# A four-layer convolution kernel: routing of the first seven images issued inside the last image's layer 2

## The chip, the core and the metric

The kernel runs on one core of one Trainium2 chip. A core has TensorE (PE in the profile, with its weight loads shown apart as PEld), VectorE (DVE), ScalarE (ACT), GpSimd (POOL) and SyncE (SP, which here only issues DMAs). Each engine takes its instructions in the order of its own queue and waits on semaphores for the others. The metric is the device time of one execution in microseconds (us); lower is better.

## What is computed

Eight images of 512 channels and 32 x 32 pixels, all in float32, go through four layers:

```
x = L0(x)   # group norm, 8-head attention, 3 steps h += 0.1*tanh(h W), projection, residual
x = L1(x)   # attention over all 1024 pixels, 64-wide q and k, residual
x = L2(x)   # upsample by 2 (12-tap FIR), leaky ReLU, downsample by 2 (12-tap FIR)
pooled = x.mean(axis=(2, 3))
rw = sigmoid(pooled @ router_w.T + router_b)            # 8 experts per image
W  = einsum('be,eoihw->boihw', rw, experts)             # each image has its own weights
x = relu(bn3(conv3(relu(bn2(conv2(relu(bn1(conv1(x, W1))), W2))), W3)) + x)
```

conv1 is 1x1 (512 to 128 channels), conv2 3x3 (128 to 128), conv3 1x1 (128 to 512). The change concerns the line with `rw`, the routing: from an image's pooled means to eight numbers that weigh the experts.

## The kernel before

Layers 0, 1 and 2 run image by image, for b = 0 to 7. Layer 3 then runs image by image over the results. Those of images 0 to 6 were spilled to DRAM at the end of their layer 2 and are loaded back by `load_z`; that of image 7 stays in SBUF.

The source gives the order in which work is issued; a scheduler then places every instruction in its engine's queue by its priority (earlier in the source is higher) and by the time at which it believes that its operands are there. So an instruction may stand in its queue well ahead of older work that is still waiting for something. Once placed, the order is fixed, and an instruction that waits holds up all that stand behind it on the same engine. Semaphores are put in automatically.

Layer 2 of an image works in eight strips t = 0 to 7 of up to nine input rows. Layer 1 writes its result `y` to a padded DRAM buffer (`ypad`, line 764: most of these DMAs are issued by ACT, the others by SP), and `halo` (line 880, SP) reads overlapping patches back. `upsample(t)` (line 920) makes four matmuls with 512 columns; each is two passes on PE in float32. `leak` follows each of them: an ACT multiplication into a small buffer (line 903), then a DVE maximum into `up` (line 904). There are two such buffers. `downsample` (line 941) makes many small matmuls on `up`. It is called three times: after strips 0 to 2, after 3 and 4, and after 5 to 7. The first call's result is copied to `z` by ACT (line 955), the second's by DVE (lines 957 and 958), the last one's by both (lines 960 and 961), and DVE then sums `z` into `pooled` (line 962).

For image 7 alone, layer 2 gets a callback, `freed(t)`, called at the end of each `downsample` with its last strip (2, 4 and 7) and with 6 ahead of the last one. Before, it does nothing for t = 2. At 4 it issues the load of the experts `w2_0` and of image 0's `z`, at 6 those of `w2_1` and `w2_2` (called w_0e, w_1e and w_2e in the profile, and w_0, w_1, w_2 here), at 7 that of `w3`. Each of these goes into a big buffer that the work just ended gives free. The experts `w1` have a buffer of their own and are loaded before.

`route(b0, b1)` (lines 1050 to 1076) computes `rw` for images b0 to b1 - 1: DVE scales `pooled` into `mean` (line 1054); PE makes four tiny matmuls `router` (line 1057, eight passes); DVE spreads the result into `apart` (line 1063); PE makes one matmul `routed` that brings it to all partitions (line 1068); DVE adds the bias (line 1072); ACT takes the sigmoid (line 1076), for which it first loads a function table. `route(0, B - 1)` is called right after its definition, ahead of image 7's layer 2 in the source. Image 7's own routing, `route(B - 1, B)`, comes behind that layer.

`mixed(b)` (lines 1087 to 1099) makes an image's weights in five parts (w1, w_0, w_1, w_2, w3): ACT multiplies the first expert (line 1094), and seven DVE steps of line 1096 add the others; a step of w1 or w3 has 512 elements per partition, one of w_0 to w_2 has 384. There are two buffers for these weights, so those of images 0 and 1 can be made as soon as their `rw` and the experts are there. The scheduler does that: `mixed(0)` and `mixed(1)` stand far behind in the source, but their w1 parts are placed as early as `rw` allows.

In layer 3 (lines 1128 to 1175) each image has matmuls c1 (line 317), c2 (line 1150) and c3 (line 1164); DVE's line 1171 takes each result of c3 out of PSUM into `z`. The pair of PSUM banks of one c3 chunk is free for the chunk after next once that has run.

Of the kernel before, what the change touches and what calls it, by code (L numbers as in the profile page):

```python
# [18 lines left out]
B, C, H, W = 8, 512, 32, 32  # L19
# [25 lines left out]
def tile_conv_sequence(tc: tile.TileContext, a: dict, out: bass.AP):  # L45


    redo = tile_sequence(tc, a, out, False)
    with tc.If(redo > 0):
        tile_sequence(tc, a, out, True)  # L50
# [3 lines left out]
def tile_sequence(ctx: ExitStack, tc: tile.TileContext, a: dict, out: bass.AP, shifted: bool):  # L54
# [15 lines left out]
    def bank(pool=None, name="mm"):  # L70
        pool = pool or ps_mm
        return pool.tile([P, HALF], F32, tag="bank", name=name)
# [823 lines left out]
    def layer2(b, halo, freed=lambda t: None):  # L896
# [32 lines left out]
        def downsample(first, last, ts_):  # L929
            for cc in range(CC):  # L930
# [28 lines left out]
                else:  # L959
# [3 lines left out]
                    if b + 1 < B:  # L963
                        nc.sync.dma_start(spilled[b][ts(cc, P), :], z[:, cc, :])
            freed(ts_[-1])

        for t in range(3):
# [10 lines left out]
        up63 = tmp(f"up63_{b}")[0 : 2 * W, :]  # L978
        leak(up63, ps, f"{b}_63")
        freed(6)  # L980
        downsample(17, 31, (5, 6, 7))
        return z
# [34 lines left out]
    def load_experts(key, n, pool=None):  # L1017
        if pool is None:
            t = big_tile(f"{key}e", [P, NE, n])
        else:  # L1020
            t = pool.tile([P, NE, n], F32, name=f"{key}e", bufs=1)
        nc.sync.dma_start(t, a[key])
        experts[key] = t

    def load_z(b):
        t = big_tile(f"z3_{b}", [P, CC, S])
        for cc in range(CC):
            nc.sync.dma_start(t[:, cc, :], spilled[b][ts(cc, P), :])
        return t
# [20 lines left out]
    def route(b0, b1):  # L1050

        n = b1 - b0
        mean = pool3.tile([P, CC, n], F32, name=f"mean_{b0}", bufs=1)
        nc.vector.tensor_scalar_mul(mean, pooled[:, :, b0:b1], 1.0 / S)
        ps = bank(ps_tp, f"router_{b0}")
        for cc in range(CC):
            nc.tensor.matmul(
                ps[0:n, 0:NE], mean[:, cc, :], router_w[:, cc, :],
                start=(cc == 0), stop=(cc == CC - 1),
            )  # L1060

        apart = pool3.tile([n, n, NE], F32, name=f"apart_{b0}", bufs=1)
        nc.vector.tensor_tensor(
            apart, ident[0:n, 0:n].unsqueeze(2).to_broadcast([n, n, NE]),
            ps[0:n, 0:NE].unsqueeze(1).to_broadcast([n, n, NE]), ALU.mult,
        )
        ps = bank(ps_tp, f"routed_{b0}")
        nc.tensor.matmul(
            ps[:, 0 : n * NE], ones[0:n, :], apart.rearrange("k b e -> k (b e)"),
            start=True, stop=True,  # L1070
        )
        nc.vector.tensor_tensor(
            rw[:, b0:b1, :], ps[:, 0 : n * NE].rearrange("p (b e) -> p b e", e=NE),
            router_b.unsqueeze(1).to_broadcast([P, n, NE]), ALU.add,
        )
        nc.scalar.activation(rw[:, b0:b1, :], rw[:, b0:b1, :], AF.Sigmoid)

    route(0, B - 1)


    rims = []
    for i in range(2):
        t = pool3.tile([P, H + 2, W + 2], F32, tag=f"rim_{i}", bufs=1, name=f"rim_{i}")
# [30 lines left out]
    z3 = {}  # L1114

    def freed(t):
        if t == 4:
            load_experts("w2_0", 3 * P)
            z3[0] = load_z(0)
        elif t == 6:  # L1120
            for ky in (1, 2):
                load_experts(f"w2_{ky}", 3 * P)
        elif t == 7:
            load_experts("w3", C)

    z_last = layer2(B - 1, halo, freed)
    z_next = z3[0]
    redo = None if shifted else out_of_bounds()
# [115 lines left out]
```

## Time and profile before

Four runs took 3938.16, 3941.11, 3941.77 and 3942.65 us; their median is 3941.44 us. The profiled execution took 3942.35 us, with a span of 3940.6 us from its first to its last instruction.

| | busy us | share of the span | instructions |
|---|---|---|---|
| PE | 3872.7 | 98% | 14630 |
| PEld | 2037.3 | 52% | 14630 |
| DVE | 2594.5 | 66% | 3690 |
| ACT | 1105.1 | 28% | 1507 |
| POOL | 435.5 | 11% | 310 |
| mean granted TensorE clock | 0.996 of full speed | | |

How to read it: PE is busy nearly all the time, so the span is PE's work plus its idle time, and an average says little about one stage. What matters here is the short stretch from about 3609 us, where image 7's layer 1 ends, to about 3750 us, in layer 3. In a row of the timeline, the first number is the start in us, the second the time to the end of the group, then engine, line, operation, tiles, shapes and count; in brackets stands how long the engine idled before it, and what ended that.

### The profile page before, as it was taken

Reading aid. Unit: us, or ns where it says so; the run is one execution under the profiler, and the core shown is the slowest. Engines: PE = TensorE matmul, PEld = TensorE weight load, DVE = VectorE, ACT = ScalarE, POOL = GpSimd, SP = SyncE. Lnnn points to the kernel's source line nnn. Section 1 sums busy time; section 2 is a strip of 40 time slices with the busy share of each in tenths; the row PEclk is TensorE's granted clock in tenths of the full one; section 3 lists DMA queues with packets and bytes.
Section 4 is the critical chain, followed back from the end, with each engine's and each line's share of the span. In section 5 each row is a group of like instructions: output and inputs, shape, how many; then the busy total and the mean of one; then the engine's idle time right before and its main releaser. Section 6 shows DMA issues by size and latency. Waiting matters only on the chain.

```text
span 3940.6 us, 37957 instructions
## 1 busy us (share of the span) xinstructions
PE 3872.7 (98%) x14630; PEld 2037.3 (52%) x14630; DVE 2594.5 (66%) x3690; ACT 1105.1 (28%) x1507; POOL 435.5 (11%) x310
## 2 busy tenths in 40 slices
PE   8999999999999999999999999999999999999998
PEld 4336653476435763366434764357534764346543
DVE  4777848764686647775586646765477655866785
ACT  1421224212332114212242123322142122421333
POOL 5310003000120003100030002200030001201000
PEclk9999999999999999999999999999999999999999
DMA  5002310122101310023101220013200131003432
GB/s 196 19 0 83 111 61 1 40 75 101 38 0 59 117 70 8 0 83 115 56 1 59 82 77 37 1 71 105 78 1 30 57 113 55 1 0 115 161 135 101
DMA packets 85792, 247.86 MB, mean 63 GB/s; under 512 B 10480, under 2 KB 33024, under 8 KB 78816
## 3 DMA queue, kind: packets, MB, share of 16 engines
q1 hardware_dynamic: 69712, 220.23, 15.7%
q10 hardware_dynamic: 13824, 12.59, 1.0%
q0 software_dynamic: 2064, 12.51, 0.8%
q8 instruction: 117, 1.92, 0.2%
q14 instruction: 75, 0.61, 0.0%
HBM read 185.40 MB, written 59.90 MB: 62 GB/s over the span
## 4 chain that ended last, share of the span: by engine, by line
PE 90%; DVE 7%; issue 1%; DMA 1%; ACT 1%; SPq 0%; POOL 0%; DVEq 0%; ACTq 0%; POOLq 0%
PE scores L266 13%; PE av L627 11%; PE inl_X L414 6%; PE dn L941 6%; PE up L920 5%; PE v_X L414 4%; PE inl_Y L414 4%; PE av_X L854 4%; PE c L1150 3%; PE v_A L414 3%; PE v_Y L414 3%; PE inl_A L414 3%; PE av_A L854 3%; PE av_Y L854 2%; PE proj_X L414 2%; PE q_X L414 2%
## 5 line engine op out<-in xcount | busy, mean ns | idle before, releaser
L612 ACT ACTIVATE e<-scores 128x1024 f32<-128x1024 f32 x512 | 497.0, 1021 | 632.7 <-PE scores L266 632.0
L618 DVE TENSOR_TENSOR acc<-acc,e 128x1024 f32<-128x1024 f32 x384 | 494.4, 1287 | 122.8 <-ACT e L612 101.7
L266 PE MATMUL scores<-q,k 64*128 64x512 f32 x2048 | 511.1, 616 | 6.9 <-ACT e L612 3.6
L627 PE MATMUL av<-e,v 128*64 128x512 f32 x2048 | 494.2, 605 | 0.0
L644 POOL TENSOR_TENSOR seen<-seen,acc 128x512 f32<-128x512 f32 x128 | 212.1, 1657 | 1578.8 <-DVE acc L618 1573.8
L266 PEld LDWEIGHTS scores<-q,k 64*128 64x128 f32 x2048 | 175.9, 186 | 334.2 <-ACT e L612 163.2
L627 PEld LDWEIGHTS av<-e,v 128*64 128x64 f32 x2048 | 124.8, 136 | 338.7 <-issue 335.7
L941 PEld LDWEIGHTS dn<-dn_op,up 128*128 128x128 f32 (+1 forms) x2048 | 241.7, 193 | 47.0 <-issue 24.3
L904 DVE SCALAR_TENSOR_TENSOR up<-up,leak 128x512 f32<-128x512 f32 (+1 forms) x264 | 175.1, 687 | 137.6 <-ACT leak L903 128.9
L941 PE MATMUL dn<-dn_op,up 128*128 128x126 f32 (+5 forms) x2048 | 246.7, 276 | 10.6 <-DVE up L904 9.9
L903 ACT ACTIVATE leak<-up 128x512 f32<-128x512 f32 (+1 forms) x264 | 150.0, 595 | 251.8 <-DVE up L904 127.2
L641 DVE RECIPROCAL inv<-total 128x512 f32<-128x512 f32 x64 | 214.7, 3355 | 0.0
L920 PE MATMUL up<-halo,up_op 126*128 126x512 f32 (+1 forms) x384 | 184.8, 611 | 0.4 <-DVE up L904 0.3
L414 PE MATMUL inl_X<-T_hf,w_inl 128*128 128x512 f32 x384 | 172.6, 592 | 0.0
L644 POOL TENSOR_TENSOR seen<-seen,inv 128x512 f32<-128x512 f32 x64 | 125.2, 1956 | 417.8 <-DVE inv L641 417.8
L414 PE MATMUL inl_A<-hf,w_inl 128*128 128x512 f32 x384 | 169.6, 595 | 0.0
L616 DVE TENSOR_TENSOR acc<-e,e 128x1024 f32<-128x1024 f32 x64 | 84.9, 1327 | 102.3 <-ACT e L612 100.6
L508 ACT ACTIVATE inl_U<-inl_U,inl_b 128x512 f32<-128x512 f32 x96 | 64.0, 714 | 304.7 <-DVE inl_U L523 304.7
L519 DVE TENSOR_TENSOR inl_U<-inl_X,inl_P 128x512 f32<-128x512 f32 x96 | 61.9, 686 | 115.9 <-PE inl_X L414 115.9
L736 POOL TENSOR_TENSOR seen<-seen,acc 128x512 f32<-128x512 f32 x16 | 22.6, 1411 | 1019.9 <-DVE acc L728 1019.9
L1150 PE MATMUL c<-rim,mixed 128*128 128x512 f32 x288 | 124.9, 592 | 0.0
L414 PEld LDWEIGHTS inl_A<-hf,w_inl 128*128 128x128 f32 x384 | 72.4, 190 | 94.4 <-issue 88.7
(302 smaller groups left out, 5764.7 us busy)
## 6 DMA issues: line engine op xcount, KB each, us to landing
halo<-ypad_u SPq DMA_DIRECT2D x128, 252.0 KB
halo<-ypad_u SPq DMA_DIRECT2D x128, 198.0 KB
w_v<-stored_u_v SPq DMA_DIRECT2D x14, 1792.0 KB
x<-in_x_dram SPq DMA_DIRECT2D x32, 512.0 KB
spill_u<-z SPq DMA_DIRECT2D x28, 512.0 KB
z<-spill_u SPq DMA_DIRECT2D x28, 512.0 KB
out_dram<-z SPq DMA_DIRECT2D x28, 512.0 KB
w_q<-stored_u_q SPq DMA_DIRECT2D x7, 1792.0 KB
```

The lines of the kernel that those rows point to most:

```text
L266: nc.tensor.matmul(ps[r], k[r], q[r], start=True, stop=(shift is None))
L414: nc.tensor.matmul(dst, lhs, rhs, start=(opens and s == 0 and cc == 0), stop=(cc == 1 and s == rows), skip_group_check=True,)
L612: nc.scalar.activation(e, ps, AF.Exp, scale=HD ** -0.5)
L618: nc.vector.tensor_add(accs[g], accs[g], e)
L627: nc.tensor.matmul(avs[g][rows[r]], v[:, jc, ts(2 * oc + r, HD)], e[:, ts(r, HALF)], start=(jc == 0), stop=(jc == SC - 1),)
L641: nc.vector.reciprocal(inv, ps)
L644: nc.gpsimd.tensor_add(seen, seen, part)
L854: nc.tensor.matmul(ps[:, ts(s, QR)], left[:, j, at : at + P], right[:, j, :], start=(what in ("P1", "U2", "W") and s == 0 and j == 0), sto ...
L904: nc.vector.scalar_tensor_tensor(dst, ps, SQRT2, t, ALU.mult, ALU.max)
L920: nc.tensor.matmul(ps[i], op[0 : IR * n, :], halo.tile(t)[0 : IR * n, c + i, :], start=True, stop=True,)
L941: nc.tensor.matmul(rows[:, r0 - first : r1 + 1 - first, c0 : c1 + 1], up[t][0:k, c, ts(cc, P)], op[:, r0 - 4 * t + 3 : r1 + 4 - 4 * t, c0 ...
L1150: nc.tensor.matmul(banks[g].rearrange("p (h w) -> p h w", w=W), wt[:, at : at + P], h1[:, ky + 16 * g : ky + 16 * g + 16, kx : kx + W], st ...
```

## The change

The call of `route` for images 0 to 6 is taken from its place behind the definition and put into the callback, under t = 2, that is behind the first `downsample` of image 7's layer 2.

```diff
         nc.scalar.activation(rw[:, b0:b1, :], rw[:, b0:b1, :], AF.Sigmoid)
 
-    route(0, B - 1)
-
 
     rims = []
@@
     def freed(t):
-        if t == 4:
+        if t == 2:
+
+            route(0, B - 1)
+        elif t == 4:
             load_experts("w2_0", 3 * P)
             z3[0] = load_z(0)
         elif t == 6:
```

`route` itself is unchanged. No operation is added or removed: the eight passes of `router`, the two of `routed`, three DVE instructions and the sigmoid with its table load are issued later. What depends on `rw`, the steps of `mixed(0)` and `mixed(1)`, is placed anew by the scheduler. In the queues that result:

- PE: `router` stood between the last matmuls of layer 1, right ahead of the first upsampling, and `routed` a few matmuls behind it. Now `router` stands between the first `downsample` and `upsample(3)`, and `routed` behind the first matmul of `upsample(3)`. The matmuls of the second `downsample` are interleaved otherwise with those of `upsample(4)` to `upsample(6)`. In layer 3, image 7's `router` stands behind all eight c1 matmuls of image 0, where it stood behind five; image 0's third and fourth c3 chunks stand behind seven of image 1's eight c1 matmuls.
- DVE: 14 steps of line 1096 for w1 (seven each of images 0 and 1) stood among the last instructions of layer 1, eight of them directly ahead of the first `leak` of layer 2. Now none stands ahead of that `leak`; between the first `leak` of strip 3 and the `mean` of image 7's routing stand ten of them, with all seven w_0 steps and all seven w_1 steps of image 0 and four of its w_2 steps. The other four w1 steps, and all of image 1's w_0 steps, stand behind that `mean`.
- ACT: the table load and the sigmoid stood ahead of two writes of `ypad`. Now they stand behind the four copies of line 955, ahead of the first `leak` of strip 3.
- SP: two writes of `ypad` stand one `halo` load earlier. POOL: the same order.

## The prediction

> **What bounds the kernel now.** I read the page first: the chain that ended last is 90% PE, so a change counts by what it does to PE's idle time or pace. Next the waits of PE:
>
> ```profile
> engine line waited for: us in total, times, longest us
> PE dn L941 <- DVE up L904: 9.9, 7, 5.6
> ...
> PE up L920 <- DMA halo<-ypad_u: 2.4, 2, 1.5
> ```
>
> Over half of the 9.9 us is one wait. The timelines of DVE and PE around it say where (two engines of one window):
>
> ```profile
> 3627.11 0.88 DVE L817 SCALAR_TENSOR_TENSOR y<-av_P,inv,y 128x256 f32<-128x256 f32 x2
> 3627.91 5.63 DVE L1096 SCALAR_TENSOR_TENSOR mixed<-w1e,rw,mixed 128x512 f32<-128x512 f32 x8
> 3633.46 0.68 DVE L904 SCALAR_TENSOR_TENSOR up<-up,leak 128x512 f32<-128x512 f32 x1
> ```
>
> ```profile
> 3625.45 3.13 PE L920 MATMUL up<-halo,up_op 126*128 126x512 f32 x6
> 3634.19 1.12 PE L941 MATMUL dn<-dn_op,up 112*128 112x66 f32 x4 [5.61 <-DVE up L904]
> 3635.61 3.78 PE L920 MATMUL up<-halo,up_op 126*128 126x512 f32 x4 [0.29 <-DVE up L904]
> 3639.18 1.92 PE L920 MATMUL up<-halo,up_left_op 99*128 99x512 f32 x2
> 3640.89 3.30 PE L920 MATMUL up<-halo,up_op 126*128 126x512 f32 x6
> ```
>
> Eight weight-mixing steps stand ahead of image 7's first leak on DVE. PE ends the upsampling that it can do and idles 5.61 us. Then it is slow: four passes with 512 columns take 3.78 us. The windows show why (length, then busy us and counts of PE, PEld, DVE, ACT, POOL; granted clock; DMA share and rate):
>
> ```profile
> 3625.00:3634.00 9.00, 3.46 (x9) 1.25 (x7) 8.93 (x15) 0.00 (x0) 0.00 (x0) 0.88 0.56 177
> 3634.00:3644.00 10.00, 9.51 (x16) 4.54 (x17) 5.49 (x9) 4.64 (x9) 0.00 (x0) 0.60 0.78 267
> 3644.00:3654.00 10.00, 10.00 (x91) 9.97 (x90) 1.98 (x3) 3.20 (x6) 0.00 (x0) 1.00 0.26 83
> ```
>
> After the idle, the granted clock is 0.60 over ten microseconds. If it is half or full, that is 8 us at half. The same stretch of image 6, which has no mixing steps:
>
> ```profile
> 3166.99 2.85 PE L920 MATMUL up<-halo,up_op 126*128 126x512 f32 x6
> 3169.67 0.56 PE L941 MATMUL dn<-dn_op,up 112*128 112x66 f32 x4
> 3170.07 1.93 PE L920 MATMUL up<-halo,up_op 126*128 126x512 f32 x4
> ...
> 3178.36 8.73 PE L941 MATMUL dn<-dn_op,up 128*128 128x126 f32 x76 [0.89 <-DVE up L904]
> 3186.92 1.05 PE L920 MATMUL up<-halo,up_left_op 99*128 99x512 f32 x2
> ```
>
> Here the downsampling follows the six passes at once, and four passes take 1.93 us.
>
> **The change, term by term.** U is the start of strip 3's upsampling on PE: 3654.28 in image 7, 3186.92 in image 6.
>
> *(a) Ahead of the stall.* `router` (0.35 us, PE at 3609.88) goes from a place where PE idles next for 1.46 us until a halo patch lands; the patch sets the start, 3611.69, so this gains nothing. `routed` (3616.18, next matmul 3616.53) stood between busy matmuls: -0.35 us. On ACT the two `ypad` writes no longer wait for the sigmoid (3617.13), but `y`, which they carry, is written at 3617.01 to 3617.89: nothing either. SP's shift by one load (0.85 us) concerns patches of strip 3, used 20 us later.
>
> *(b) The stall.* From the six passes to U: image 7 takes 3654.28 - 3625.45 = 28.83 us. The same instructions take 18.77, 19.33, 20.07, 19.24 and 19.93 us in images 1, 2, 3, 5 and 6 (U minus the start of the six passes), mean 19.47. Image 4 takes 22.59 (rivals). After the change image 7 has the same instructions there: -9.36 us, bounds -8.8 and -10.1. By parts: 5.61 idle; 3634.19 to 3635.61 against 3169.67 to 3170.07, 1.02 more; twelve passes in 3635.61 to 3644.03, 8.42 us against 5.34 in image 6, 3.08 more; together 9.7, less the short waits (0 to 0.9) that images 1 to 6 have later. Nearly 4 us of this is no wait but half rate.
>
> [...]
>
> *(c) Routing at its new place.* `router` and `routed` now stand between busy matmuls: 0.25 (eight passes about 0.03 apart) and 0.35 us, +0.6. PE's trip over DVE to `routed` is covered by the first upsampling matmul (0.86). ACT's table load (1.28) runs behind the last z copy, while PE waits on neither; the sigmoid waits for `routed` and DVE's addition, and strip 3's first leak stands behind it. Leak starts at U + 1.94 now (3656.22) and some 0.3 later then; PE has seven more passes to do: +0.05.
>
> *(d) Fourteen w1 steps elsewhere.* Interleaved they are 0.665 us apart (four in 2.73), in all 9.3 us on DVE. Their cover has to be DVE's idle time in layer 2:
>
> ```profile
> 3656.85:3696.26 39.41, 38.76 (x214) 27.36 (x213) 32.50 (x59) 16.01 (x30) 0.00 (x0) 1.00 0.54 194
> ...
> 3696.26:3720.72 24.46, 24.45 (x65) 10.50 (x64) 23.25 (x42) 5.20 (x8) 0.00 (x0) 1.00 0.27 110
> ```
>
> The first row runs from strip 3's first leak to image 7's `mean`; DVE is busy 32.50 of 39.41 us. Its list changes by +10 w1, +3 w_2 and -4 of image 1's w_0 (0.53 each): 6.65 + 1.6 - 2.1 = +6.1 us, against 6.9 us idle. Set one by one in the new order, the steps fill about 4 us of that idle (the 0.66 us waits of DVE on ACT above all) and push `mean` back about 2.1 us, to U + 44.5 with the 0.3 of (c). PE wanted it for `router` at U + 43.47 (3697.75); it now has three more c1 matmuls ahead (3 x 0.86) and the 0.6 of (c): U + 46.6. It waits for nothing, by about 2 us. Next, `routed` of image 7 comes five c2 matmuls (4.3 us) later; DVE then needs 4 x 0.665 + 3 x 0.53 = 4.25 us to reach `apart`: the same slack. The first w3 step moves from `mean` + 4.2 to `mean` + 1.2, while w3e lands at U + 44.8 (3699.10) and ACT's first step takes 0.7: ready at U + 45.5, wanted at U + 45.7, so DVE may idle a few tenths. Last, DVE's way from `mean` to c3's first result (3718.86, U + 64.6) grows by four w1 and four w_0 steps of image 1 less three w_2 of image 0, 3.2 us, less its 1.2 idle: with the 2.4 above, U + 69.0, and 1.28 for itself. PE wants the banks that it frees after four c3 and seven c1 matmuls, 11 x 0.86 behind U + 62.4 (3716.67) + 0.6: U + 72.5. From the third image DVE has 2 to 3 us idle in each 29.5 us and catches up. Bounds: 0 and 9.3 us. I take +0.4, near the lower end, since every place has slack by these rows.
>
> Sum: -0.35 - 9.36 + 0.65 + 0.4 = -8.66 us. Against the profiled execution's 3942.35 that is 3933.7; it lies 0.91 above the median of the runs, 3941.44, which gives **3932.8 us**.
>
> **Rivals.**
> 1. *Half the clock gain is missing.* Image 4 had waits of 0.92 and 0.89 us at U - 11.6 and - 10.2, and its 76 small matmuls took 10.36 instead of 8.73 us. If image 7 gets such a dip, (b) is 28.83 - 22.59 = 6.24, and the time 3932.8 + 3.1 = 3935.9. For it: image 7's strip patches land as late as image 4's. Against: one image of six. A run of before that escaped the half rate (3938.16 may be one) would show the same smaller gain, but three of four lie above 3941. [...]
> 2. *DVE becomes the late engine at one of the three places of (d)*, costing 3 to 5 us: about 3937. For: it is 95% busy in the second row above. Against: the slack worked out.
> 3. *Slower: DVE takes the stall over.* If the filled idle is not there, all 9.3 us meet PE at `router` or `routed` of image 7; a wait that long halves the clock again, +3.6: 3932.8 - 0.4 + 9.3 + 3.6 = 3945.3. It decides once `mean` is later than U + 46.6 by more than about 8 us. Against: it needs all the idle time to stay unused, though the steps stand between the leaks.
> 4. *The stall stays*, because the first leak waits for something else just behind the steps: 3941.4. Against: in images 1 to 6 the leak follows `y` on DVE at once (3166.97 + 0.80 = 3167.77).
>
> **Chances and range.** Forecast 0.67 (3930.5 to 3935), rival 1 0.12, rival 2 0.12, rival 3 0.06, rival 4 0.03. A difference of 0.2%, 7.9 us, is about what a measurement of this kernel can tell from no change; it lies 0.8 us inside the forecast, which I put beyond it four times in five: faster 0.54. Within: the rest of the forecast, rivals 1, 2 and 4 and a third of 3: 0.42. Slower by more: 0.04, if the delay of rival 3 also reaches image 1. The range reaches over rivals 1 and 2: 3929 to 3938.5.
>
> **What would show it.** In the profile after: no wait above 1 us of PE's L941 on DVE's L904 at image 7; granted clock 1.00 over the ten microseconds behind that place; about 19.5 us from the six passes to U; `router` between the 92 small matmuls and U; DVE above 95% busy from U to layer 3's second image; no PE wait above 1 us at image 7's `router` and `routed`, at L1150 or at the third c3 chunk of image 0. It is wrong if the clock dips there again, if L904 still comes late, or if a wait of several us appears at the start of layer 3.

## The result, and the profile after

The changed kernel takes 3932.05 us (median of 32 runs, 3927.23 to 3937.61). The kernel before, over all of its 52 runs, takes 3939.95 us (3932.88 to 3948.08). The ratio is 0.9981, with a 95% interval from 0.9976 to 0.9986: 5.5 to 9.5 us less (the medians differ by 7.90), where the prediction had 8.66. (It was made against the 3941.44 us of the four runs shown; against 3939.95 the same sum gives 3931.3.) The profiled execution took 3931.28 us, with a span of 3929.5.

PE's waits in the changed kernel, by the line that waited and what it waited for (the same view as before):

```profile
engine line waited for: us in total, times, longest us
...
PE dn L941 <- DVE up L904: 2.4, 4, 0.9
...
PE up L920 <- DMA halo<-ypad_u: 2.3, 2, 1.8
```

The 5.6 us wait of the first downsampling is gone; no wait of L941 on a leak is above 0.9 us. PE's timeline from image 7's first patch to strip 3:

```profile
3607.59 1.10 PE L920 MATMUL up<-halo,up_left_op 99*128 99x512 f32 x2 [1.80 <-DMA halo<-ypad_u]
...
3622.67 2.93 PE L920 MATMUL up<-halo,up_op 126*128 126x512 f32 x6
3625.44 0.56 PE L941 MATMUL dn<-dn_op,up 112*128 112x66 f32 x4
3626.55 1.99 PE L920 MATMUL up<-halo,up_op 126*128 126x512 f32 x4 [0.55 <-DVE up L904]
...
3632.05 10.51 PE L941 MATMUL dn<-dn_op,up 112*128 112x84 f32 x92
3642.48 0.35 PE L1057 MATMUL router<-router_w,mean 128*7 128x8 f32 x8
3642.76 1.12 PE L920 MATMUL up<-halo,up_left_op 99*128 99x512 f32 x2
3643.82 0.42 PE L1068 MATMUL routed<-apart,ones 7*128 7x56 f32 x2
3644.17 2.84 PE L920 MATMUL up<-halo,up_op 126*128 126x512 f32 x6
```

The downsampling follows the six passes at once, four passes take 1.99 us instead of 3.78, and `router` stands between the 92 small matmuls and U, the start of strip 3. From the six passes to U it is 3642.76 - 3622.67 = 20.09 us instead of 28.83. DVE around the same place shows why:

```profile
3623.60 0.88 DVE L817 SCALAR_TENSOR_TENSOR y<-av_P,inv,y 128x256 f32<-128x256 f32 x2
3624.40 0.68 DVE L904 SCALAR_TENSOR_TENSOR up<-up,leak 128x512 f32<-128x512 f32 x1
```

The leak follows the last `y` with no mixing step between. The windows behind (columns as before) have the clock at 1.00, where before had 0.60:

```profile
3625.00:3634.00 9.00, 8.45 (x35) 4.83 (x34) 6.22 (x11) 5.72 (x11) 0.00 (x0) 1.00 0.78 254
3634.00:3644.00 10.00, 10.00 (x88) 9.11 (x88) 1.26 (x3) 3.45 (x6) 0.00 (x0) 1.00 0.81 262
```

The two profiled spans differ by 11.07 us, more than the medians do. Three stretches add up to it. Up to image 7's first upsampling matmul (3611.69 before, 3607.59 after) nothing was changed but that `router` no longer stands just ahead of it, in a wait of PE, and the 4.10 us there are chance: in e1 to e6 of the experiments this point, with the same work ahead of it, lies anywhere from 3605.65 to 3615.40. From there to U, which I call the ruler below, before takes 42.59 us and after 35.18 (the last digit is rounded in the rows): 7.41 less. From U to the end it is 286.28 and 286.73: 0.45 more. So the change itself gave 6.96 us in this pair of profiles.

### The profile page after: what moved, and what is told of

Read it like the earlier page. It is cut to its first block, busy times and chain, and to the rows that moved or that the text cites. A ratio compares the mean times of both kernels' runs of the same rounds, so it can differ in the third digit from the quotient of the medians.

```text
span 3929.5 us, 37961 instructions
## 1 busy us (share of the span) xinstructions
PE 3870.4 (98%) x14630; PEld 2034.6 (52%) x14630; DVE 2593.1 (66%) x3690; ACT 1105.1 (28%) x1507; POOL 435.6 (11%) x310
## 4 chain that ended last, share of the span: by engine, by line
PE 91%; DVE 6%; issue 1%; DMA 1%; ACT 1%; SPq 0%; POOL 0%; ACTq 0%; DVEq 0%; POOLq 0%
PE scores L266 13%; PE av L627 11%; PE inl_X L414 6%; PE dn L941 6%; PE up L920 5%; PE v_X L414 4%; PE inl_Y L414 4%; PE av_X L854 4%; PE c L1151 3%; PE v_A L414 3%; PE v_Y L414 3%; PE inl_A L414 3%; PE av_A L854 3%; PE av_Y L854 2%; PE proj_X L414 2%; PE q_X L414 2%
## 5 line engine op out<-in xcount | busy, mean ns | idle before, releaser
L941 PEld LDWEIGHTS dn<-dn_op,up 128*128 128x128 f32 (+1 forms) x2048 | 241.8, 193 | 40.2 <-issue 25.2
L941 PE MATMUL dn<-dn_op,up 128*128 128x126 f32 (+5 forms) x2048 | 246.2, 276 | 3.1 <-DVE up L904 2.4
L854 PE MATMUL av_X<-v,eT 128*128 128x256 f32 x512 | 120.6, 384 | 1.8 <-DVE av_W L833 1.0
```

Source lines behind the costliest of these rows:

```text
L854: nc.tensor.matmul(ps[:, ts(s, QR)], left[:, j, at : at + P], right[:, j, :], start=(what in ("P1", "U2", "W") and s == 0 and j == 0), sto ...
L941: nc.tensor.matmul(rows[:, r0 - first : r1 + 1 - first, c0 : c1 + 1], up[t][0:k, c, ts(cc, P)], op[:, r0 - 4 * t + 3 : r1 + 4 - 4 * t, c0 ...
```

## The experiments

"Half-clock record" in the expectations means a stretch for which the trace records the granted clock at 0.5. Within one profile such records start on multiples of 3.413 us from each other (the last section has the places); the stretch of 3.41 us from one such multiple to the next is called a window here.

### What makes the stall: the mixing steps or the routing itself

e1 leaves the routing at its old place and holds only the mixing: the steps of `mixed` read `rw_held`, a copy of `rw` that waits for image 7's first downsampled rows (a column of them, times zero, is added). In the code shown here, `@@` stands for lines left out.

```diff
     route(0, B - 1)
@@ def mixed(b):
+        rwb = rw_held if b < B - 1 else rw
@@ layer2, behind each downsample
+            if b == B - 1 and first == 0:
+                n = (B - 1) * NE
+                nc.vector.scalar_tensor_tensor(
+                    rw_held[:, 0 : B - 1, :].rearrange("p b e -> p (b e)"),
+                    z[:, CC - 1, 0:n], 0.0,
+                    rw[:, 0 : B - 1, :].rearrange("p b e -> p (b e)"), ALU.mult, ALU.add,
+                )
             freed(ts_[-1])
```

> The routing of images 0 to 6 is called where it was before the change; only the weight mixing is held: it reads a copy of rw that DVE makes from image 7's first downsampled rows (times zero, added). Ruler: from image 7's first upsampling matmul to U, the start of strip 3's upsampling (before 42.59 us, after 35.17 us, of which about 1.3 us stand under one half-clock record of 3.41 us). Theory (the mixing steps on DVE alone make the stall): 33.2 us (13.76 of before up to the six passes, with routed inline, plus 19.47), up to 34.9 with one half-clock record; no PE wait above 1 us on a leak; time 3929 to 3935, as after. Rival A (the place of router, routed or the table load matters by itself): the 5.6 us wait is still there, ruler 42.6, time about 3940.

Measured: 3930.8 us against 3939.41 of the kernel before, ratio 0.998 (0.997 to 0.9989). PE's timeline of e1:

```profile
3607.14 0.35 PE L1065 MATMUL router<-router_w,mean 128*7 128x8 f32 x8
3608.93 1.10 PE L920 MATMUL up<-halo,up_left_op 99*128 99x512 f32 x2 [1.43 <-DMA halo<-ypad_u]
...
3622.68 2.93 PE L920 MATMUL up<-halo,up_op 126*128 126x512 f32 x6
3625.45 0.56 PE L941 MATMUL dn<-dn_op,up 112*128 112x66 f32 x4
...
3642.40 1.04 PE L920 MATMUL up<-halo,up_left_op 99*128 99x512 f32 x2
```

The ruler is 33.48 us (33.2 expected) with `router` at its old place. So the stall is the mixing steps' alone, and rival A falls. The row of `router` shows one thing more: there it fills part of the patch's wait, and PE idles 1.43 us instead of the 1.80 in the changed kernel.

### How much of it was the clock

e2 gives PE something to do in the old stall. DVE keeps its 14 steps; the extra results are overwritten.

```diff
+                if b == B - 1 and first == 0 and cc == 0:
+                    for _ in range(6):
+                        nc.tensor.matmul(ps, up_op[0 : IR * IC, :],
+                            halo.tile(1)[0 : IR * IC, 2, :], start=True, stop=True)
                 blocks = [(t, c) for t in ts_ for c in range(4)]
```

> The kernel before, with six more upsampling matmuls of 512 columns (each two passes, 6 x 0.86 = 5.2 us) that write the bank of image 7's first downsampling, whose own first matmul then starts it anew: PE has work in the 5.61 us, DVE is as before. Theory (nearly 4 of the 9.4 us are the clock at half, brought about by PE's idle time): no half-clock record near image 7's first downsampling, ruler 42.59 - 3.1 to 3.6 = 39.0 to 39.5 us, time 3936.5 of a median 3940. Rival B (the passes behind the stall are slow for another reason, such as the patches' transfers at a DMA share of 0.78): ruler 42.2 to 42.6 us, time as before.

PE's timeline of e2 (its L936 are the added passes, L947 is the downsampling):

```profile
3623.65 1.02 PE L920 MATMUL up<-halo,up_op 126*128 126x512 f32 x2
...
3627.09 4.45 PE L936 MATMUL dn<-halo,up_op 126*128 126x512 f32 x10
3632.40 0.66 PE L947 MATMUL dn<-dn_op,up 112*128 112x66 f32 x4 [0.85 <-DVE up L904]
3633.81 1.99 PE L920 MATMUL up<-halo,up_op 126*128 126x512 f32 x4 [0.76 <-DVE up L904]
```

From the first of the six passes to the first downsampling it is 3632.40 - 3623.65 = 8.75 us, in before 3634.19 - 3625.45 = 8.74: the stall on DVE is untouched, but PE is busy 7.90 us of these 8.75, at a granted clock of 1.00. Yet from that downsampling to the end e2 takes 302.14 us (3934.54 - 3632.40) and before 306.36 (3940.55 - 3634.19), and no half-clock record lies there. Transfers are no cause: in the ten us behind, their share is 0.80 in e2 and 0.78 in before. So 4.22 us of the price were the half rate (3.1 to 3.6 expected), brought about by PE's own idle time; PE's wait behind that downsampling is even 0.47 us longer in e2 (0.76 against 0.29). The ruler itself is no measure for e2, since the scheduler put U ahead of a part of the small matmuls; and the timed median, 3937.35 against 3939.41 (ratio 0.9993, 0.9983 to 1.0003), can't tell the 4 us from nothing. This reading rests on the two profiles.

### The price of a shorter stall

e3 and e4 lengthen the first leak of the changed kernel.

```diff
+            for _ in range(3 if name == f"{B - 1}_0_0" else 1):   # e4: 5
                 nc.vector.scalar_tensor_tensor(dst, ps, SQRT2, t, ALU.mult, ALU.max)
```

> The changed kernel; image 7's very first leak on DVE is issued three times instead of once (same operands, same result), 2 x 0.665 = 1.33 us more ahead of the first downsampling. Theory: some 0.3 us are covered, PE idles 0.9 to 1.1 us, the clock stays at full; ruler (35.17 - 1.3 for the half-clock record of after = 33.9) 34.9 us. Rival C (any wait near 1 us halves the clock, as the two of 0.9 us in image 4 did): 36.6 us with a record of 3.41 us.

> As the last, with four more leaks, 2.66 us. Theory (the clock halves where PE was idle over half of a free-running window of 3.41 us; the records of before and after start at multiples of 3.413 us from each other): PE idles 2.3 us, ruler 36.2 us at full clock, and in about two of three cases one record of 3.41 us more, 37.9 us. Rival D (a stall always brings three windows, 10.24 us, as before): 39.8 us. Rival E (the price is the idle time alone): 36.2 us and no record in any case.

| | DVE work added | from the six passes to U | PE idle in it | half-clock record behind |
|---|---|---|---|---|
| after | 0 | 20.09 | 0.55 | none |
| e3 | 1.33 us | 22.91 | 0.98 + 0.76 | 3.41 us |
| e4 | 2.66 us | 24.19 | 2.43 + 0.76 | 3.41 us |
| before (no `router` in it) | eight steps | 28.83 | 5.61 + 0.29 | 10.24 us |

e4 came out as the theory had it (ruler 37.59, 37.9 expected). e3 did not: 36.30, close to rival C's 36.6, where I expected 34.9. I had counted the first wait alone. The windows of e3 on both sides of the halving:

```profile
3629.27:3632.68 3.41, 1.71 (x7) 1.09 (x8) 2.15 (x4) 1.56 (x3) 0.00 (x0) 1.00 0.85 260
3632.68:3636.09 3.41, 3.41 (x6) 1.30 (x5) 2.67 (x4) 2.08 (x5) 0.00 (x0) 0.50 0.79 266
```

In the first of them PE is busy 1.71 us of 3.41, because the waits of 0.98 and 0.76 us both fall into it; the next runs at half throughout. So two more leaks, 1.33 us, cost 2.82. Rival D (always three windows) and E (idle time alone) fall with e4. Single runs, 3937.22 and 3941.11 us, say little here: both had 6.83 us at half clock in image 5 (from 2721.32 and 2723.91), in code that no edit touches.

### How much room DVE has for the steps

e5 and e6 issue the routing later still, behind the second and behind the last downsampling.

```diff
     def freed(t):
-        if t == 2:
-            route(0, B - 1)
-        elif t == 4:
+        if t == 4:              # e6: t == 7, behind load_experts("w3", C)
+            route(0, B - 1)
```

> The changed kernel, with the routing of images 0 to 6 issued behind image 7's second downsampling instead of the first, ahead of the loading of w2_0. Rulers: from image 7's first upsampling to U (after 35.18 us with a half-clock record, held mixing 33.48 without), and from U to the end (286.3 to 286.7 in before, after and the held mixing). Theory (DVE has some us of idle time left in layer 2 and at the start of layer 3, and they run out if the steps come later): first ruler 33.2 (34.6 with a record), the second 289, 2.3 us more, by setting the steps one by one in the new order; PE waits of 1 us and more where image 7's layer 2 ends. Rival F (there is room wherever the steps stand): second ruler 287.0 or less. Rival G (all 14 steps show, 9.3 us): 296.

> The same with the routing issued behind image 7's last downsampling, so that none of the mixing lies in layer 2. Theory: PE waits some 8 us for mixed_0 at the first c1 matmul of layer 3 and some 2 us at image 0's third c3 chunk, the clock halves behind the first, second ruler 286.5 + 12.3 + 3 to 4 = 302 us, time 3946 to 3949, slower than the kernel before. Rival F: second ruler 287, time 3931.

e5: ruler 33.12, from U to the end 289.34 (289 expected); 3930.14 us in one run. PE's timeline at the end of image 7's layer 2 in e5:

```profile
3671.75 0.68 PE L949 MATMUL dn<-dn_op,up 64*128 64x96 f32 x4 [0.33 <-DVE up L904]
3673.81 2.90 PE L941 MATMUL dn<-dn_op,up 128*128 128x99 f32 x24 [1.38 <-ACT z L961]
```

There a wait of 0.65 in the changed kernel has become 1.38 us. The room is real but ends about here: F and G both fall. e6, with no mixing in layer 2:

```profile
3680.66 0.59 PE L1068 MATMUL routed<-apart,ones 1*128 1x8 f32 x2 [0.24 <-DVE apart L1063]
3689.37 8.74 PE L317 MATMUL c<-z,mixed 128*128 128x512 f32 x16 [8.11 <-issue]
```

Layer 3's first matmul waits 8.11 us for its weights (the view names no releaser), as expected. But from U to the end e6 takes 298.35 us, not 302: the second wait, at the third c3 chunk, did not come, and the 3 to 4 us for the half rate were too many: of 13.65 us at half clock from 3679.02 on, PE idled through 9.40 (1.05, 0.24 and 8.11). The single run took 3938.92 us, about the time of the kernel before (3938.46) instead of the 3946 to 3949 expected; its image 7 happens to start early, at 3605.65. Rival F falls.

### The same kind of stall in image 0

Image 0 has a wait like the one removed, in both kernels (PE in the changed kernel):

```profile
420.48 2.74 PE L920 MATMUL up<-halo,up_op 126*128 126x512 f32 x6
429.68 0.59 PE L296 MATMUL gn_var<-gdev,group_mean 128*128 128x4 f32 x2 [6.46 <-DVE gdev L294]
430.13 2.05 PE L920 MATMUL up<-halo,up_left_op 99*128 99x512 f32 x2
```

6.46 us idle, and 6.83 us at half clock, from 427.46 on. DVE is building `layer2_constants` there, and the steps behind `dn_op` serve only the last rows of the image. e7 holds these until the first downsampled rows exist; e8 does the same on top of e1.

```diff
-            layer2_constants()
+            layer2_constants(False)          # up_op, up_left_op, dn_op
@@
-                layer2(b, halo)
+                layer2(b, halo, lambda t, b=b: b == 0 and t == 2 and layer2_constants(True))
@@ layer2_constants(True): up63_op, dn63_op, in scratch of their own
+            nc.vector.scalar_tensor_tensor(
+                part, made["z"][:, CC - 1, 0:1], 0.0, part, ALU.mult, ALU.add
+            )
```

> The changed kernel, and the same move in image 0: the DVE steps that build the two operators of the last rows (up63_op, dn63_op), which stand ahead of the group norm's gdev and of image 0's first leak, are held until image 0's first downsampled rows are there (their index is added to zero times those). In after PE waits 6.46 us there and 6.83 us stand at half clock. Theory (it is the same kind of stall): from image 0's first upsampling to its strip 3 21.5 to 23 us instead of 30.30, no half-clock record at 427 us, time 3932 - 7.5 to 8.8 = 3923 to 3925. Rival H (image 0's patches or the group norm itself are late anyway): 27 us and more, time 3929 to 3932.

> The kernel with the held mixing (routing at its old place, mixing steps held by the copy of rw), with the last rows' operators of image 0 held as well. Theory: as the run before less up to 1 us, since router fills part of the patch's wait at image 7's first strip (1.43 us of idle instead of 1.80, which half the time is followed by a half-clock record worth 1.4 us) and stands no more among busy matmuls: 3922 to 3924. Rival: the same as the run before.

e7 takes 3937.9 us and e8 3939.01 against 3938.46 of the kernel before (ratios 0.9994, 0.9984 to 1.0004, and 0.9999, 0.999 to 1.0009): the gain of the change is lost again. PE in e7:

```profile
441.44 1.05 PE L926 MATMUL up<-halo,up_left_op 99*128 99x512 f32 x2
...
451.27 1.17 PE L947 MATMUL dn<-dn_op,up 128*128 128x99 f32 x4 [4.49 <-DVE setup L177]
...
481.29 0.94 PE L947 MATMUL dn<-dn_op,up 128*128 128x77 f32 x4 [1.31 <-DVE up L910]
483.65 2.08 PE L420 MATMUL q_X<-T_h,w_q 128*128 128x512 f32 x2 [1.42 <-DVE T_h L385]
```

The first stall did go (23.19 us from image 0's first upsampling, at 418.24, to strip 3 at 441.44; 30.30 in the changed kernel). But the held steps now stand ahead of strip 3's leaks (4.49 us), and later among the image's last leaks and the next image's `h` and `T_h` (1.31 and 1.42 us). At each of these two places 6.83 us at half clock follow, from 450.81 and from 481.53; the second record begins behind the wait of 1.31 us, and the one of 1.42 falls into it. Image 1's first upsampling comes at 883.67 instead of 876.94. Neither my theory nor rival H had this: it is the prediction's rival 3, a stall taken over by DVE at a later place, and here it happened.

So the steps have to leave DVE's queue. e9 and e10 give them to POOL, called in image 0's layer 0; e11 and e12 hold them there until the attention's last result `hf` exists (e10 and e12 on top of e1).

```diff
+        if b == 0:
+            layer2_constants(nc.gpsimd, hf)      # e9, e10: True instead of hf
         for it in range(3):
@@ layer2_constants, e11 and e12
+            eng.tensor_scalar_mul(wait, last_rows[:, CC - 1, S - 1 : S], 0.0)   # last_rows is hf
+            eng.tensor_add(part, part, wait)
```

> The changed kernel; the steps that build image 0's last-row operators run on POOL instead of DVE, called in image 0's layer 0, behind the scores, in a scratch tile of their own. Run e7 took the 6.46 us wait away (23.19 us from image 0's first upsampling to strip 3 against 30.30) but the held steps came back as waits of 4.49 us at strip 3's leaks and over 4 us at the next image's q, with two stretches at half clock. Theory (those steps only have to leave DVE's queue in these 80 us): 23.2 us in image 0 as in e7, image 1's first upsampling 457.4 us behind image 0's first upsampling less 7.1 = 450.3, time 3932 - 7 = 3925 (3923.5 to 3926.5). Rival I (POOL is slow with some 150 small steps, or delays the weight sums behind them): the 7 us are lost again in image 0's layer 0 or 1, time 3930 to 3940.

> The same on the kernel with the routing at its old place and the mixing steps held. Theory: as e9, less up to 1 us: 3924 (3922.5 to 3926). Rival: the same as e9 or slower.

e9 takes 3956.33 us and e10 3954.23 against 3941.5 (1.0039, 1.0025 to 1.0053, and 1.0038, 1.0025 to 1.0052). This is rival I: the scheduler placed the ready steps at once. One row each of PE, ACT and POOL in e9:

```profile
135.65 3.78 PE L268 MATMUL scores<-q,k 64*128 64x512 f32 x8 [28.05 <-ACT e L614]
134.58 1.94 ACT L614 ACTIVATE e<-scores 128x1024 f32<-128x1024 f32 x2 [31.50 <-POOL w_v L361]
133.28 1.26 POOL L361 TENSOR_TENSOR w_v<-w_v,raw_v 128x512 f32<-128x512 f32 x1
```

PE waits for ACT's exponential, and that starts as soon as POOL's step of line 361 ends. This step belongs to the sums that POOL makes of the parts of the weights `w_v`, and is the last to read the scratch tile `raw_v`; the exponential's result `e` takes a scratch tile of the same kind. In the changed kernel these sums run from 93.67 to 101.40 us; in e9 POOL works on the new steps from 49 to 118 us and begins the sums at 126.39. The next expectation puts the wait down to POOL's adds to `seen`, but the first of these comes at 141.86, behind the wait.

> As e9 (the changed kernel, image 0's last-row operators built on POOL), but POOL's steps are held until the last group of hf is there (their index gets zero times a column of it added), some 230 us into the span. In e9 they ran at 48 us, ahead of POOL's adds to seen that free the sums, and PE waited 28.1 us for an exponential; image 0's ruler was 23.27. POOL idles for 118 us behind the scores, and the 154 steps took some 0.2 to 0.4 us each: 45 to 60 us. Theory: 23.2 us for image 0's ruler, no wait above 1 us for an exponential, image 1's first upsampling 876.94 - 7.1 = 869.9, time 3925 (3923.5 to 3926.5). Rival J (DVE and POOL disturb each other, or the 7 us come back as another wait in image 0's layer 1 or 2): 3928 to 3932.

> The same on the kernel with the routing at its old place and the mixing steps held. Theory: 3924 (3922.5 to 3926), image 7's ruler 33.5 (35.2 with a half-clock record). Rival: the same as e11 or slower.

e11 takes **3923.08 us** against 3938.16, ratio 0.9964 (0.995 to 0.9977), and e12 3925.13, 0.9965 (0.9951 to 0.9979). PE in image 0 of e11:

```profile
419.81 1.88 PE L928 MATMUL up<-halo,up_op 126*128 126x512 f32 x4
421.52 0.30 PE L301 MATMUL gn_var<-gdev,group_mean 128*128 128x4 f32 x2
...
431.74 10.51 PE L949 MATMUL dn<-dn_op,up 112*128 112x84 f32 x92
442.08 1.04 PE L928 MATMUL up<-halo,up_left_op 99*128 99x512 f32 x2
```

No wait at `gn_var`, 23.21 us to strip 3 and image 1's first upsampling at 868.81 instead of 876.94. POOL works off the steps, 190 and not the 154 expected, between 231.46 and 310.83 us, busy 67.6 us of these 79.4, where nothing on the way to image 0's first upsampling waits for it (418.87 us, against 419.55 in the changed kernel). This version is ahead of the kernel before by 15.1 us in the medians, clear of the noise, where the change alone had 7.9. That would put it some 7 us ahead of the changed kernel; the two intervals barely overlap (0.9976 and 0.9977), but the two were not timed against each other. Holding the mixing on top of it (e12) gives nothing that these runs can tell.

## Why the prediction was right, and where it was off

**(a) Ahead of the stall: -0.35 forecast, wrong in this profile.** From the first upsampling to the six passes before takes 13.76 us, the changed kernel's profile 3622.67 - 3607.59 = 15.08. The part of `routed` is right: where the clock stays full, e3 takes 13.39 and e1, with `routed` inline, 13.75. What the step "so this gains nothing" left out is the clock behind the patch's wait. The patch still sets the start, but without `router` ahead of it PE idles 1.80 us instead of 1.46, and here all of it fell into one clock window:

```profile
3605.27:3608.68 3.41, 1.61 (x6) 0.76 (x5) 2.75 (x6) 0.00 (x0) 0.00 (x0) 1.00 0.66 218
3608.68:3612.10 3.42, 3.42 (x10) 2.72 (x9) 0.00 (x0) 0.00 (x0) 0.00 (x0) 0.50 0.78 241
3612.10:3615.51 3.41, 3.41 (x14) 2.35 (x14) 1.57 (x3) 0.60 (x1) 0.00 (x0) 1.00 0.70 247
```

The window behind runs at half, which costs 15.08 - 13.39 = 1.69 us. It is a matter of chance: of the eight profiles without `router` at its old place, three (after, e9, e11) have this record, of the six with it one (e8); the 16 passes behind the patch take 5.31 us in after and 5.30 in e11, 3.62 in before. These counts are too few to show that the place of `router` has a part in it. Without the record the pair of profiles would differ by 6.96 + 1.69 = 8.65 us from this point on, against the forecast 8.66. That they agree so closely is luck: (b) gained some 0.3 us less than forecast and (d) cost some 0.3 us less.

**(b) The stall: -9.36 forecast, right.** 28.83 became 20.09 with 0.28 of `router` in it, so 19.81: -9.02, inside the bounds of -8.8 and -10.1; a wait of 0.55 us is left. That "nearly 4 us of this is no wait but half rate" was read from durations alone; e2 measures 4.22. The trace of before has three windows at 0.50, from 3631.77 to 3642.01: in the first PE is still waiting (busy 0.99 us of 3.41), in the second it waits 0.29 us, and the third is fully busy (3.41); the next is at 1.00.

**(c) Routing at its new place: +0.6 on PE forecast, 0.63 measured** (3642.76 - 3642.48 = 0.28 and 3644.17 - 3643.82 = 0.35). Strip 3's first leak starts on ACT at U + 2.6 (3645.39) instead of the forecast 2.2, and PE waits for nothing by it.

**(d) Fourteen steps elsewhere: +0.4 forecast, 0.1 measured.** From U to the end it is 0.45 us more, of which `routed` is 0.35. The 0.1 left is less than chance moves: in e3, e4, e7, e9 and e11, which have the routing at the same new place, this stretch takes 286.12 to 287.01 us. The windows of the changed kernel from strip 3's first leak on DVE to image 7's `mean`, and from there on into layer 3:

```profile
3646.02:3688.43 42.41, 41.76 (x222) 28.68 (x221) 38.55 (x69) 17.91 (x33) 0.00 (x0) 1.00 0.54 198
3688.43:3710.33 21.90, 21.89 (x60) 9.40 (x59) 21.90 (x42) 3.77 (x6) 0.00 (x0) 1.00 0.18 71
```

DVE's idle time shrank from 6.9 to 3.9 us in the first and from 1.2 to none in the second, which is what was to pay for the steps. From U to layer 3's second image (3709.37) it is busy 59.91 of 66.61 us, 90%, not the 95% and more that I had named. Each place held, some more narrowly than forecast: eleven w1 steps, and not ten, stand ahead of `mean`, which comes at U + 45.7 (44.5 forecast) with `router` wanted at U + 46.6, DVE's first c3 result at U + 70.0 (69.0) with its banks wanted at U + 72.6. The waits of PE from U to 3760 us are one:

```profile
PE dn L941 <- ACT z L961: 0.7, 1, 0.7
```

e5 and e6 show that the cover was not free of limits: from U to the end it takes 2.6 us more (289.34 - 286.73) if the steps start one downsampling later, and 11.6 more if they start behind layer 2; 0.28 us of each is `router`, which then stands behind U.

**The rivals.** Rival 1's half-clock dip did come, but at the patch ahead of the six passes instead of at the small matmuls, and only in some of the profiles. Rivals 2, 3 and 4 did not; rival 3 is what e7 ran into. The +3.6 us for the clock in rival 3 is an estimate, 1.02 + 3.08 of (b) less its short waits; no run shows that figure, and what e2 showed in its place is 4.22.

## What to carry to other kernels

A dependent step that is ready early may be placed ahead of work that PE needs; to move it, take away its readiness (a real data dependence, or a later producer), and look first for idle time of that engine, or another engine, that can hold all of it: the same kind of move gained some 8 us in image 7, nothing in image 0 while the work stayed on DVE, and some 7 us there once POOL had it (868.81 - 418.87 = 449.94 us from image 0's first upsampling to image 1's, 457.39 in the changed kernel). Count a PE stall of a few us nearly double where the clock halves behind it: here 5.61 us idle cost 4.22 us more. Whether a tiny operation that shortens a wait, as `router` did at its old place, is worth its place there by keeping the clock up was not shown.

## What the runs showed of the clock

Within one profile the records of half clock start on multiples of 3.413 us from each other: in before at 426.66, 2266.44 and 3631.77 (539 and 400 windows apart), in after at 427.46, 2263.83 and 3608.68 (538 and 394), in e3 at 2721.32 and 3632.68 (267), in e4 at 2723.91 and 3635.27 (267), in e7 at 450.81 and 481.53 (9). Of those in before, the first and the last start while PE waits, the second while it is busy with small matmuls. They last 3.41, 6.83 or 10.24 us, in e6 13.65 (before and after also have one that the kernel's end cuts off). What I had not expected is how little idle time stands ahead of a window at half. I set the idle time of PE in each window at full clock against the clock of the next, leaving the first 25 us out. Among long matmuls (256 or 512 columns) the next window was at 1.00 behind 1.69 us of idle time (before, from 27.30) and at 0.50 behind 1.80 (after, from 3605.27); behind 1.88 at the end of before (from 3928.73, where the last matmul ends) it was at 1.00. Among the small downsampling matmuls it was at 1.00 behind 0.88 (after, from 1806.45) and at 0.50 behind 1.33 (after, from 2260.42) and 1.81 (before, from 2263.03). Where long matmuls and smaller ones mix, the clock halved behind 1.70 (e3, from 3629.27) and behind 0.85 with `router` and `routed` among the last downsampling matmuls (e6, ahead of 3679.02). So about half a window of idle time, and less among small matmuls, stood ahead of a half-clock record here; where the line runs between these figures was not shown. In image 4 of before, the 1.81 us are waits of 0.92 and 0.89 us in one window, and the 76 small matmuls behind took 10.36 us; in image 6 one wait of 0.89 fell into two windows (0.33 and 0.56), and they took 8.73. That such records come in some executions and not in others may be one source of the spread between runs of one kernel; this was not measured. Why less idle time was enough among the small matmuls was not tried.
